# Normalized rows sent to the experts, projection by chunks and softplus by halves in the first block

## The chip, the cores and the metric

The kernel runs on one core of a Trainium2 chip. The metric is the device time of one execution in microseconds (us), the median over several. The core has five engines that run their own instruction streams in order: PE (matrix products, with weight loads shown as PEld), DVE, ACT, POOL and SP, of which SP only issues transfers here. They wait for each other on semaphores.

## The reference, cut to what matters

The input is four sequences of 1024 tokens with 512 channels. A state-space layer and a mixture of eight experts follow one another, each behind a layer norm that is modulated by per-sequence vectors, and each added back with a gate. In short:

```python
mod = silu(c) @ wmod                  # per sequence: sa, ca, ga, sb, cb, gb
h = layernorm(x) * (1 + ca) + sa
u = causal_conv(h, 4 taps) + conv_b
dt, Bm, Cm = split(u @ xproj_w.T)     # 128 + 16 + 16 columns
delta = softplus(dt @ dtproj_w.T + dtproj_b)
# 16 states per channel, step by step over the tokens
s = exp(delta * A) * s + delta * Bm * u
y = sum(s * Cm) + u * D_skip
x = x + ga * y
h = layernorm(x) * (1 + cb) + sb
logits = tanh(h @ Wg1.T) @ Wg2.T      # two of eight experts a token, softmax of the two
out = sum over both of score * (silu(h @ Wup[e].T + bup[e]) @ Wdown[e].T + bdown[e])
x = x + gb * out
```

All is 32-bit floating point.

## The kernel before, in words

**Blocks.** The tokens are cut into nine blocks (`BLOCKS`): seven of 512 tokens, then one of 384 and one of 128, the last sequence being cut 512, 384, 128. Token tiles have 128 rows; the 512 channels are four chunks (`dc`). A block goes through three parts.

*Front* (`front`): rows are loaded, normalized, turned channel-first with PE transposes, modulated (`turned`, `affine`: multiply by one column, add another) and convolved on DVE (`conv`). `u` is the convolution's output, one chunk after another. The projection `u @ xproj_w.T` (L716) gives 160 columns for each token tile; two tiles share a bank of PSUM. It is done tile by tile, each over the four chunks, and the planner's step waits for all chunks. Then `pre(dc)` makes the parts of the softplus with Abs, Exp and Identity on ACT, and one step does the four `Ln` (L838) when all four chunks are there. `post(dc)` multiplies delta by u and turns the product token-first (`duT`).

*Scan.* For each of 16 states and four chunks a unit is run: `products_b` (dB, ACT or POOL), `inputs` (PE transposes to `pb`), `decays` (Exp on ACT, L916), `recurrences` (the scan on DVE, L946), `products_c` (hc on POOL, L963), `sums` (PE, accumulated in the two banks `acc0` and `acc1`, L1002). That makes 576 units.

*Back* (`back`): the second norm on rows (`second_norm`: `xn`, token-first, and `h2T`, turned and modulated), the router on `h2T`, and positions for both choices of each token in a table of rows in DRAM, ordered by expert. `scatter(t)` turns the modulated `h2T` back to rows (L1316), copies them twice, on ACT (L1320) and on DVE (L1324), puts the score of a choice into column 512 of each copy (L1326), and writes each with an indirect transfer from POOL (L1331). Once a group's rows have landed, `tiles` loads tiles of 128 rows and the weights of their expert (1 MB each), and `expert` computes: rows turned channel-first (L1403), one copy to `xT` (helper `copy`, L347 on ACT or L349 on DVE), up product (L1416), bias, Tanh, product, down product (L1444), scaled by score and gate (L1454), stored back in place. `combine` gathers both results of each token (L1493) and adds. There are six groups of blocks (`GROUPS`), 86 tiles in all. The last block of 128 tokens goes through all eight experts densely (`dense`).

**The order.** All parts are generators. A planner written in Python (`Order`) runs them when the program is built: each `yield step(engine, cost, dependencies)` is placed where its engine is free and its inputs are there by assumed costs (`t_mm`, `t_act`, `t_dve`, `t_pool`), and due times (`DUE`, `TILES_DUE`) break ties. What it decides is the fixed order of every engine's instructions; `either` lets it choose DVE or ACT for an operation. Buffers are rings (`ring(tag, n)`): `t512B` has four row buffers, shared by `xn` and by the copies for the scatter. A cost in the planner is an assumption: it changes the order alone.

The scatter's issue as it stands:

```python
yield step(POOL, 1.2, copied, kb=256)
nc.gpsimd.tensor_copy(idx[:, k, t : t + 1], to[:, k, t : t + 1])
i = nc.gpsimd.indirect_dma_start(out=xs_d[g], out_offset=..., in_=h2[k].t, in_offset=None)
```

Of the kernel before, what the change touches and what calls it, by code (L numbers as in the profile page):

```python
# [14 lines left out]
P = 128  # L15
# [5 lines left out]
DC = D // P  # L21
# [254 lines left out]
def adaln_mamba_moe_kernel(  # L276
# [232 lines left out]
    def mod_part(s):  # L509
        if s >= 3:  # L510
# [3 lines left out]
            wm_in[s].t = o.fin  # L514
        yield step(PE, t_mm(512), banks, wm_in[s])
        pm, tag = new_bank(f"pm_{s}")
        for kc in range(DC):
            if kc:
                yield step(PE, t_mm(512))
            nc.tensor.matmul(  # L520
                pm[:B, :],
                lhsT=sc[:, kc, :],
                rhs=wm_sb[s].t[:, kc * D : (kc + 1) * D],
                start=(kc == 0),
                stop=(kc == DC - 1),
            )
# [115 lines left out]
    def front(blk):  # L642
# [61 lines left out]
        bT = Buf("bT", 2, [P, NT, NS], f"bT_{blk}")  # L704
        bT_sb[blk] = bT
        for t2 in range(0, nt, 2):
            w = min(2, nt - t2)
            yield step(PE, t_mm(XP, DC), banks, gated_in[b], *u_in)
            if t2 == 0:
                hT.done()  # L710
            px, tag = new_bank(f"pxd_{blk}_{t2}")
            for i in range(w):
                if i:
                    yield step(PE, t_mm(XP, DC))
                for kc in range(DC):
                    nc.tensor.matmul(  # L716
                        px[:, i * XP : (i + 1) * XP],
                        lhsT=u(kc)[:, (t2 + i) * P : (t2 + i + 1) * P],
                        rhs=xpg[b].t[:, kc, :],
                        start=(kc == 0),  # L720
                        stop=(kc == DC - 1),
                    )
            yield either(w * XP, 1)
            copy(xd.t[:, t2 : t2 + w, :].rearrange("p t w -> p (t w)"), px[:, : w * XP])
            yield step(DVE, 0.15)
            nc.vector.tensor_copy(
                bT.t[:, t2 : t2 + w, :], px[:, : w * XP].rearrange("p (t w) -> p t w", w=XP)[:, :, R : R + NS]
            )
            banks.give(tag, o.fin)
        if t0 + n == L:  # L730
# [19 lines left out]
        y_in = [Event() for _ in range(DC)]  # L750
        ln_in = Event()

# [25 lines left out]
        def post(dc):  # L778
            yield step(both(n), None, ln_in, y_in[dc], ring("t512A", 4))
            dd = delta[dc // 2].t[:, dc % 2, :n]  # L780
# [33 lines left out]
        for dc in range(2):  # L814
            o.spawn(pre(dc), due0 + 60.0 + 4.0 * dc, 3.0)

        yield step(PE, t_tr(nt), banks, ring("t512A", 4))
# [16 lines left out]
        for dc in range(2, DC):  # L834
            o.spawn(pre(dc), due0 + 60.0 + 4.0 * dc, 3.0)
        yield step(ACT, t_act(n, DC) + 2.6, *y_in)
        for dc in range(DC):
            nc.scalar.activation(y.t[:, dc, :n], y.t[:, dc, :n], AF.Ln, bias=1.0)  # L838
        ln_in.t = o.fin
        for h in range(2):  # L840
            yield step(POOL, 0.01, ring("duT", 3), after=[])
            duT.append(Buf("duT", 3, [P, NT, 2 * P], f"duT_{blk}_{h}"))
            for dc in range(2 * h, 2 * h + 2):
                o.spawn(post(dc), due0 + 95.0 + 4.0 * dc, 3.0)

# [310 lines left out]
    def second_norm(blk):  # L1156
        b, t0, n = BLOCKS[blk]
        nt = n // P
        x1_in = [event("x1", blk, dc) for dc in range(DC)]
        yield step(POOL, 0.01, ring("wideB", 1), ring("t512B", 4).many(nt), *x1_in)  # L1160
        h2T = wide("B", f"h2T_{blk}")
        xn = [t512("B", f"xn_b{blk}_{t}", DC) for t in range(nt)]
        yield from layernorm([[half.t[:, t, :] for half in xr[blk]] for t in range(nt)], xn, x1_in[-1], f"b{blk}", "B")
        h2_in = [Event() for _ in range(DC)]

        def turn(dc):
            yield from turned(xn, n, dc, b, 3, 4, h2T.t[:, dc, :n], f"b{blk}")
            h2_in[dc].t = o.fin

        for dc in range(DC):  # L1170
            o.spawn(turn(dc), DUE[blk + 1] + 8.0 + 2.0 * dc + LAST[blk], 2.0)
        return h2T, h2_in

    def back(blk):
# [4 lines left out]
        if b not in gbh:  # L1179
            yield from gate(b)  # L1180
        hb, h2_in = yield from second_norm(blk)
        h2T = hb.t[:, :, :n]
        rank, sv, s_all = yield from router(blk, h2T, h2_in)
        routed = Event()
# [116 lines left out]
        nc.vector.tensor_tensor(to, to, posf, ALU.add)  # L1301
        yield step(POOL, 0.55)
        idx = tl(blk, "idx", [P, 2, NT], I32, bufs=2)
        idx_sb[blk] = tl(blk, f"idx{blk}", [P, 2, NT], I32)
        nc.gpsimd.tensor_scalar(idx_sb[blk][:, :, :nt], posf, Z, None, ALU.min)
        idx_rest[blk] = tl(blk, f"idr{blk}", [P, 2, NT], I32)
        nc.gpsimd.tensor_scalar(idx_rest[blk][:, :, :nt], to, Z, None, ALU.max)
        xs_d[g] = xs_buf[g % N_XS]
        left = [nt]

        def scatter(t):
            yield step(PE, t_tr(DC), banks, ring("t512B", 4).many(2), combined[g - N_XS])
            h2 = [t512("B", f"h2_{blk}_{t}_{k}") for k in range(2)]
            ph, tag = new_bank(f"ph_{blk}_{t}")
            for dc in range(DC):
                nc.tensor.transpose(ph[:, dc * P : (dc + 1) * P], h2T[:, dc, t * P : (t + 1) * P], ident)  # L1316
            turned_in = Event()
            turned_in.t = o.fin
            yield step(ACT, t_act(512))
            nc.scalar.copy(h2[0].t[:, :D], ph)  # L1320
            copied = Event()
            copied.t = o.fin
            yield step(DVE, t_dve(512) + 0.15, after=[turned_in])
            nc.vector.tensor_copy(h2[1].t[:, :D], ph)  # L1324
            for k in range(2):
                nc.vector.tensor_copy(h2[k].t[:, D:], sv[:, k, t : t + 1])  # L1326
            banks.give(tag, o.fin)
            for k in range(2):
                yield step(POOL, 1.2, copied, kb=256)
                nc.gpsimd.tensor_copy(idx[:, k, t : t + 1], to[:, k, t : t + 1])  # L1330
                i = nc.gpsimd.indirect_dma_start(  # L1331
                    out=xs_d[g],
                    out_offset=bass.IndirectOffsetOnAxis(ap=idx[:, k, t : t + 1], axis=0),
                    in_=h2[k].t,
                    in_offset=None,
                )
                apart(f"token{g}", i)
                h2[k].done()
            left[0] -= 1
            if left[0] == 0:  # L1340
                hb.done()
                scattered[g][0] -= 1
# [52 lines left out]
    def expert(g, j, xs, w, left):  # L1395
# [6 lines left out]
        for dc in range(DC):  # L1402
            nc.tensor.transpose(px[:, dc * P : (dc + 1) * P], xs.t[:, dc * P : (dc + 1) * P], ident)  # L1403
        yield either(512, 1)
        copy(xT.t.rearrange("p c t -> p (c t)"), px)
        banks.give(tag, o.fin)
# [105 lines left out]
    def dense(blk):  # L1512
# [3 lines left out]
        for tag in ("acc0", "acc1"):  # L1516
            banks.give(tag, o.fin)
        hb, h2_in = yield from second_norm(blk)
        h2T = hb.t[:, :, :n]
# [207 lines left out]
```

## Time and profile before

| | us |
|---|---|
| median of 3 runs (lowest, highest) | 1458.58 (1455.88, 1464.79) |
| the profiled execution | 1464.0 |
| its span, from the first instruction to the last | 1462.3 |
| first scan begins | 65.0 |
| last scan ends | 1383.2 |
| busy PE / DVE / ACT / POOL | 1231.8 / 1145.7 / 1045.8 / 1045.1 |
| granted TensorE clock, mean over the span | 0.925 |

An engine's busy time is the time in which it works on at least one instruction. Lines such as `L353 ACT ACTIVATE hT<-pt_a,mod 128x128 ... x4 | 1.7, 449 | 2.2` give the line of the program, the engine, the operation, output and inputs, shape and count, then the group's busy time in us and the mean duration of one in ns, then the idle time of the engine just before and what ended it. In a timeline the first two numbers are start and duration in us; brackets hold the wait before, and what ended it. `SPq` is the transfer queue of SP.

### The profile page before, as it was taken

What the parts mean: (1) busy time and instruction counts of PE and PEld (TensorE: products, weight loads), DVE (VectorE), ACT (ScalarE), POOL (GpSimd) and SP (SyncE); (2) the same over time, 40 slices, a digit from 0 to 9 for tenths busy, and PEclk for the clock granted to TensorE, in tenths of its full rate; (3) what the DMA queues carried; (4) which work ended last, traced back from release to release, by engine and by line L of the source; (5) the groups of instructions that cost most, each with busy time, mean ns of one, the idle gap of its engine ahead of it and who ended that gap; (6) DMA issues with size and microseconds to landing.
All of it is one profiled execution on the core that took longest, in us unless ns stands there. A gap on an engine that the chain in (4) does not pass through costs nothing. (4 is left out here: it accounts for less than half of the span.)

```text
span 1462.3 us, 24472 instructions
## 1 busy us (share of the span) xinstructions
PE 1231.8 (84%) x7716; PEld 929.7 (64%) x7716; DVE 1145.7 (78%) x1861; ACT 1045.8 (72%) x2095; POOL 1045.1 (71%) x1241
## 2 busy tenths in 40 slices
PE   5588778877779989997879989998899899987886
PEld 2447565655568767775667757776677767753563
DVE  4569989898988789998896869898879888656343
ACT  2779898689778676899686766896789868444320
POOL 1468987798788567897796657787788878656222
PEclk8799988889899999999798999999999999996798
DMA  4357663847599999653788976777999978966997
GB/s 176 112 158 158 120 170 83 210 109 205 124 271 281 284 266 253 216 144 97 200 280 279 289 219 209 248 248 199 290 281 286 282 196 318 339 182 158 343 311 206
DMA packets 141935, 321.65 MB, mean 220 GB/s; under 512 B 14899, under 2 KB 43475, under 8 KB 128998
## 3 DMA queue, kind: packets, MB, share of 16 engines
q1 hardware_dynamic: 111344, 254.35, 57.0%
q0 software_dynamic: 13888, 32.58, 10.4%
q10 hardware_dynamic: 16566, 33.08, 8.9%
q8 instruction: 63, 1.03, 0.3%
q14 instruction: 74, 0.61, 0.1%
HBM read 245.95 MB, written 82.40 MB: 225 GB/s over the span
## 5 line engine op out<-in xcount | busy, mean ns | idle before, releaser
L963 POOL TENSOR_TENSOR hc<-h,cq 128x512 f32<-128x512 f32 (+2 forms) x576 | 685.1, 1259 | 184.0 <-PE acc L1002 57.1
L888 ACT ACTIVATE dB<-duT,bT 128x256 f32<-128x256 f32 x820 | 368.1, 499 | 85.3 <-PE pb L931 79.9
L931 PE MATMUL pb<-ident,dB 128*128 128x128 f32 x2048 | 348.1, 293 | 82.5 <-DVE h L946 66.9
L916 ACT ACTIVATE h<-delta,a_neg 128x512 f32<-128x512 f32 (+2 forms) x576 | 369.7, 666 | 61.1 <-POOL state L971 30.7
L1002 PE MATMUL acc<-ident,hc 128*128 128x128 f32 x2048 | 340.4, 291 | 69.0 <-POOL hc L963 67.0
L946 DVE TENSOR_TENSOR_SCAN h<-h,state,pb 128x512 f32<-128x512 f32 (+2 forms) x320 | 330.4, 1054 | 50.3 <-PE pb L931 24.9
L931 PEld LDWEIGHTS pb<-ident,dB 128*128 128x128 f32 x2048 | 252.5, 150 | 171.1 <-DVE h L946 86.2
L1002 PEld LDWEIGHTS acc<-ident,hc 128*128 128x128 f32 x2048 | 251.2, 148 | 153.9 <-POOL hc L963 110.0
L946 DVE TENSOR_TENSOR_SCAN h<-h,pb 128x512 f32<-128x512 f32 x256 | 303.5, 1208 | 51.7 <-PE pb L931 32.3
L1444 PE MATMUL po<-w,hid 128*128 128x512 f32 x344 | 182.7, 621 | 9.9 <-DVE hid L1436 9.8
L1416 PE MATMUL pe<-xT,w 128*128 128x128 f32 x1376 | 183.9, 278 | 3.4 <-ACT xT L347 3.4
L1416 PEld LDWEIGHTS pe<-xT,w 128*128 128x128 f32 x1376 | 170.2, 193 | 25.8 <-issue 13.3
L895 POOL TENSOR_TENSOR dB<-duT,bT 128x512 f32<-128x512 f32 (+1 forms) x108 | 109.4, 1044 | 30.5 <-PE pb L931 24.6
L1493 POOL DMA_INDIRECT xc<-xs,idx x56 | 90.3, 1613 | 44.9 <-DMA xc<-xs,idx 18.3
L1454 DVE SCALAR_TENSOR_TENSOR xs<-po,xs,gbh 128x512 f32<-128x512 f32 x86 | 63.8, 742 | 42.9 <-PE po L1444 42.6
L1331 POOL DMA_INDIRECT xs<-h,idx x62 | 63.5, 1024 | 35.1 <-POOL idx L1330 12.3
L1434 ACT ACTIVATE th<-pe 128x256 f32<-128x256 f32 x86 | 32.5, 378 | 66.1 <-DVE pe L1427 65.6
L1444 PEld LDWEIGHTS po<-w,hid 128*128 128x128 f32 x344 | 55.4, 198 | 26.1 <-issue 16.6
L347 ACT COPY xT<-px 128x512 f32<-128x512 f32 x81 | 46.7, 578 | 31.8 <-PE px L1403 31.6
L971 POOL COPY state<-h 128x2 f32<-128x2 f32 x160 | 56.0, 350 | 0.0
L1403 PE MATMUL px<-ident,xs 128*128 128x128 f32 x344 | 54.4, 283 | 1.2 <-DVE delta L774 1.2
L1427 DVE TENSOR_TENSOR pe<-pe,w 128x256 f32<-128x256 f32 x86 | 36.1, 420 | 22.9 <-PE pe L1416 19.3
(200 smaller groups left out, 1523.2 us busy)
## 6 DMA issues: line engine op xcount, KB each, us to landing
w<-w_all SPq DMA_DIRECT2D x86, 1025.0 KB, 9.4
cq<-scr SPq DMA_DIRECT2D x224, 256.0 KB, 4.8
xs<-xs SPq DMA_DIRECT2D x86, 256.5 KB, 5.3
xs<-xs SPq DMA_DIRECT2D x86, 256.0 KB, 8.3
xs<-xc ACTq DMA_DIRECT2D x16, 1026.0 KB, 9.9
we<-w_all SPq DMA_DIRECT2D x8, 1025.0 KB, 14.5
xf<-in_x SPq DMA_DIRECT2D x32, 256.0 KB, 5.6
xr<-in_x SPq DMA_DIRECT2D x14, 512.0 KB, 10.7
```

What stands on the lines that cost most here:

```text
L888: nc.scalar.activation(dB[u // 2].t[:, t, :], duT_sb[blk][half].t[:, t, :], AF.Identity, scale=bT_sb[blk].t[:, t, n : n + 1],)
L895: engine().tensor_tensor(dB[u // 2].t[:, t0:t1, :], duT_sb[blk][half].t[:, t0:t1, :], bT_sb[blk].t[:, t0:t1, n].unsqueeze(2).to_broadcast( ...
L916: nc.scalar.activation(hs[u // 2].t[:, i, :ln], delta_sb[blk][half].t[:, i, :ln], AF.Exp, scale=a_neg[:, dc, n : n + 1])
L931: nc.tensor.transpose(pbs[u][:, t * P : (t + 1) * P], dB[u // 2].t[:, t, i * P : (i + 1) * P], ident)
L946: nc.vector.tensor_tensor_scan(h, h, pbs.pop(u)[:, :ln], 0.0 if t0 == 0 else state[:, n, dc : dc + 1], ALU.mult, ALU.add,)
L963: nc.gpsimd.tensor_tensor(hcs[u].t[:, :ln], hs[u // 2].t[:, i, :ln], cq[u // 2].t[:, :ln], ALU.mult)
L1002: nc.tensor.matmul(acc[blk, dc][:, t * P : (t + 1) * P], lhsT=src.t[:, t * P : (t + 1) * P], rhs=ident, is_transpose=True, start=False, st ...
L1331: i = nc.gpsimd.indirect_dma_start(out=xs_d[g], out_offset=bass.IndirectOffsetOnAxis(ap=idx[:, k, t : t + 1], axis=0), in_=h2[k].t, in_off ...
L1416: nc.tensor.matmul(pu[:, hc * P : (hc + 1) * P], lhsT=up[:, kc, hc * P : (hc + 1) * P], rhs=xT.t[:, kc, :], start=(kc == 0), stop=(kc == D ...
L1444: nc.tensor.matmul(po, lhsT=hid.t[:, hc * P : (hc + 1) * P], rhs=w.t[:, W_DN + hc * D : W_DN + (hc + 1) * D], start=(hc == 0), stop=(hc == ...
L1454: nc.vector.scalar_tensor_tensor(xs.t[:, :D], po, xs.t[:, D:], gbh[b].t, ALU.mult, ALU.mult)
L1493: nc.gpsimd.indirect_dma_start(out=a, out_offset=None, in_=xs_d[g], in_offset=bass.IndirectOffsetOnAxis(ap=idx_sb[blk][:, choice, t : t + ...
```

## The change

Three things are changed.

1. In the first block the projection loops over channel chunks outside and token tiles inside: each chunk is used as soon as its convolution is done. It accumulates in the two banks `acc0` and `acc1`, which the scans do not use yet. Also, the planner's cost of the first modulation product (`s == 0`) is doubled.
2. In the first block `Ln` is done for two halves of the channels, each with its own event, and the `post` of a half is started behind it. In all blocks the `Ln` of several chunks is one instruction: 1024 columns in the first block, 2048 in the others (fewer in short blocks).
3. The rows that are scattered are the normalized rows `xn` themselves. The turn back, both copies and the small index casts go. POOL writes the score of a choice into column 512 of `xn` and issues the transfer, for choice 0 and then for choice 1 from the same buffer. The index table is cast once a block. In `expert` the modulation is applied when the turned tile is copied to `xT`: four `affine` operations of 128 columns in place of one copy of 512. `xn` is held until it is scattered, `h2T` only until the router is done.

The diff, cut to its core:

```diff
@@ mod_part
-        yield step(PE, t_mm(512), banks, wm_in[s])
+        slow = 2 if s == 0 else 1
+        yield step(PE, t_mm(512, slow), banks, wm_in[s])
...
@@ front
+        pxs = []
+        if blk == 0:
+            for t2 in range(0, nt, 2):
+                pxs.append(psum.tile([P, 512], F32, tag=f"acc{t2 // 2}", name=f"pxd_{blk}_{t2}"))
+            for kc in range(DC):
+                yield step(PE, t_mm(XP, nt), gated_in[b], u_in[kc])
+                for t in range(nt):
+                    nc.tensor.matmul(
+                        pxs[t // 2][:, t % 2 * XP : (t % 2 + 1) * XP],
+                        lhsT=u(kc)[:, t * P : (t + 1) * P],
+                        rhs=xpg[b].t[:, kc, :],
+                        start=(kc == 0 and t % 2 == 0),
+                        stop=(kc == DC - 1 and t % 2 == 1),
+                    )
...
+        LN = 2 if blk == 0 else 1
+        ln_in = [Event() for _ in range(LN)]
+
+        def logs(k):
+            c0, c1 = k * DC // LN, (k + 1) * DC // LN
+            yield step(ACT, t_act(n * (c1 - c0)) + 2.6, *y_in[c0:c1])
+            nc.scalar.activation(y.t[:, c0:c1, :n], y.t[:, c0:c1, :n], AF.Ln, bias=1.0)
+            ln_in[k].t = o.fin
+
+        def posts(h):
+            yield step(POOL, 0.01, ring("duT", 3), after=[])
+            duT.append(Buf("duT", 3, [P, NT, 2 * P], f"duT_{blk}_{h}"))
+            for dc in range(2 * h, 2 * h + 2):
+                o.spawn(post(dc), due0 + 95.0 + 4.0 * dc, 3.0)
...
+        if LN == 2:
+            o.spawn(logs(0), due0 + 64.0, 3.0)
+            yield from posts(0)
...
-        yield step(ACT, t_act(n, DC) + 2.6, *y_in)
-        for dc in range(DC):
-            nc.scalar.activation(y.t[:, dc, :n], y.t[:, dc, :n], AF.Ln, bias=1.0)
-        ln_in.t = o.fin
...
+        yield from logs(LN - 1)
+        for h in range(LN - 1, 2):
+            yield from posts(h)
@@ second_norm
-        xn = [t512("B", f"xn_b{blk}_{t}", DC) for t in range(nt)]
+        xn = [t512("B", f"xn_b{blk}_{t}", DC + (blk + 1 < NBLK)) for t in range(nt)]
@@ back
-        yield step(POOL, 0.55)
+        yield step(POOL, 0.8)
...
+        nc.gpsimd.tensor_copy(idx[:, :, :nt], to)
...
         def scatter(t):
-            yield step(PE, t_tr(DC), banks, ring("t512B", 4).many(2), combined[g - N_XS])
-            h2 = [t512("B", f"h2_{blk}_{t}_{k}") for k in range(2)]
...
-                nc.tensor.transpose(ph[:, dc * P : (dc + 1) * P], h2T[:, dc, t * P : (t + 1) * P], ident)
...
-            nc.scalar.copy(h2[0].t[:, :D], ph)
...
-            nc.vector.tensor_copy(h2[1].t[:, :D], ph)
             for k in range(2):
-                nc.vector.tensor_copy(h2[k].t[:, D:], sv[:, k, t : t + 1])
...
-                yield step(POOL, 1.2, copied, kb=256)
-                nc.gpsimd.tensor_copy(idx[:, k, t : t + 1], to[:, k, t : t + 1])
+                yield step(POOL, 1.3, combined[g - N_XS], kb=256)
+                nc.gpsimd.tensor_copy(xn[t].t[:, D:], sv[:, k, t : t + 1])
                 i = nc.gpsimd.indirect_dma_start(
...
-                    in_=h2[k].t,
+                    in_=xn[t].t,
...
@@ expert
-        yield either(512, 1)
-        copy(xT.t.rearrange("p c t -> p (c t)"), px)
+        yield either(P, DC)
+        for dc in range(DC):
+            affine(xT.t[:, dc, :], px[:, dc * P : (dc + 1) * P], mcol(4, dc, b), mcol(3, dc, b))
```

More of the change, by code (lines that the diff above doesn't have):

```diff
@@ L518, in mod_part @@
             if kc:
-                yield step(PE, t_mm(512))
+                yield step(PE, t_mm(512, slow))
             nc.tensor.matmul(
@@ L705, in front @@
         bT_sb[blk] = bT
+        pxs = []
[12 more added lines that the diff above has]
+                    )
+            hT.done()
+            pxs_in = Event()
+            pxs_in.t = o.fin
         for t2 in range(0, nt, 2):
             w = min(2, nt - t2)
[L708 to L712, printed above, removed]
+            if blk:
+                yield step(PE, t_mm(XP, DC), banks, gated_in[b], *u_in)
+                if t2 == 0:
+                    hT.done()
+                px, tag = new_bank(f"pxd_{blk}_{t2}")
+            else:
+                px = pxs[t2 // 2]
+            for i in range(w if blk else 0):
                 if i:
@@ L722, in front @@
                     )
-            yield either(w * XP, 1)
+            if blk:
+                yield either(w * XP, 1)
+            else:
+                yield either(w * XP, 1, after=[pxs_in])
             copy(xd.t[:, t2 : t2 + w, :].rearrange("p t w -> p (t w)"), px[:, : w * XP])
@@ L728, in front @@
             )
-            banks.give(tag, o.fin)
+            if blk:
+                banks.give(tag, o.fin)
         if t0 + n == L:
@@ L750, in front @@
         y_in = [Event() for _ in range(DC)]
-        ln_in = Event()
+        LN = 2 if blk == 0 else 1
[10 more added lines that the diff above has]
+                o.spawn(post(dc), due0 + 95.0 + 4.0 * dc, 3.0)
         def pre(dc):
@@ L778, in post @@
         def post(dc):
-            yield step(both(n), None, ln_in, y_in[dc], ring("t512A", 4))
+            yield step(both(n), None, ln_in[dc * LN // DC], y_in[dc], ring("t512A", 4))
             dd = delta[dc // 2].t[:, dc % 2, :n]
@@ L835, in front @@
             o.spawn(pre(dc), due0 + 60.0 + 4.0 * dc, 3.0)
-        yield step(ACT, t_act(n, DC) + 2.6, *y_in)
-        for dc in range(DC):
-            nc.scalar.activation(y.t[:, dc, :n], y.t[:, dc, :n], AF.Ln, bias=1.0)
-        ln_in.t = o.fin
[L840 to L844, printed above, removed]
+        yield from logs(LN - 1)
+        for h in range(LN - 1, 2):
+            yield from posts(h)
     UNITS = []
@@ L1171, in second_norm @@
             o.spawn(turn(dc), DUE[blk + 1] + 8.0 + 2.0 * dc + LAST[blk], 2.0)
-        return h2T, h2_in
+        return h2T, h2_in, xn
     def back(blk):
@@ L1180, in back @@
             yield from gate(b)
-        hb, h2_in = yield from second_norm(blk)
-        h2T = hb.t[:, :, :n]
-        rank, sv, s_all = yield from router(blk, h2T, h2_in)
+        hb, h2_in, xn = yield from second_norm(blk)
+        rank, sv, s_all = yield from router(blk, hb.t[:, :, :n], h2_in)
+        hb.done()
         routed = Event()
@@ L1311, in scatter @@
         def scatter(t):
-            yield step(PE, t_tr(DC), banks, ring("t512B", 4).many(2), combined[g - N_XS])
-            h2 = [t512("B", f"h2_{blk}_{t}_{k}") for k in range(2)]
[L1314 to L1324, printed above, removed]
-            for k in range(2):
-                nc.vector.tensor_copy(h2[k].t[:, D:], sv[:, k, t : t + 1])
-            banks.give(tag, o.fin)
-            for k in range(2):
-                yield step(POOL, 1.2, copied, kb=256)
-                nc.gpsimd.tensor_copy(idx[:, k, t : t + 1], to[:, k, t : t + 1])
+            for k in range(2):
+                yield step(POOL, 1.3, combined[g - N_XS], kb=256)
+                nc.gpsimd.tensor_copy(xn[t].t[:, D:], sv[:, k, t : t + 1])
                 i = nc.gpsimd.indirect_dma_start(
@@ L1337, in scatter @@
                 apart(f"token{g}", i)
-                h2[k].done()
+            xn[t].done()
             left[0] -= 1
             if left[0] == 0:
-                hb.done()
                 scattered[g][0] -= 1
@@ L1517, in dense @@
             banks.give(tag, o.fin)
-        hb, h2_in = yield from second_norm(blk)
+        hb, h2_in, _ = yield from second_norm(blk)
         h2T = hb.t[:, :, :n]
```

## The prediction

> **What bounds the kernel now.** I read the page first, then busy time by stretches, then groups by form, then the timeline of the start and of the end.
>
> ```profile
> span 1462.3 us, 24472 instructions
> PE 1231.8 (84%) x7716; PEld 929.7 (64%) x7716; DVE 1145.7 (78%) x1861; ACT 1045.8 (72%) x2095; POOL 1045.1 (71%) x1241
> ```
>
> Four engines lie between 71% and 84%: no single one bounds the whole. The stretches below run from the first scan of a half block to that of the next (columns: span, then busy time of PE, PEld, DVE, ACT, POOL, clock, DMA).
>
> ```profile
> 193.00:270.00 77.00, 59.15 (x352) 44.04 (x352) 70.52 (x124) 64.19 (x125) 60.52 (x69) 0.88 0.49 118
> ...
> 574.00:641.00 67.00, 62.95 (x446) 51.56 (x445) 62.10 (x73) 57.99 (x112) 56.99 (x49) 1.00 0.74 221
> 641.00:722.00 81.00, 65.71 (x385) 47.22 (x383) 71.22 (x133) 65.72 (x131) 63.99 (x84) 0.87 0.49 125
> ...
> 908.00:975.00 67.00, 64.37 (x456) 52.35 (x455) 61.30 (x71) 59.66 (x117) 52.71 (x44) 1.00 0.77 240
> ...
> 1069.00:1137.00 68.00, 63.05 (x446) 52.74 (x445) 60.11 (x72) 61.06 (x127) 61.19 (x63) 0.95 0.91 278
> ```
>
> Two kinds are seen. Where a block's second half (norm, router, scatter) runs and almost no expert tile does (193 to 270, 332 to 411, 641 to 722), DVE is fullest, 70.5 of 77. Where expert tiles run, PE is, 63 to 64 of 67, and ACT stands at 58 to 61. From 65 to 1383 us scans follow one another with four pauses over 10 us (20 the longest), so what the start saves and what each stretch saves adds up.
>
> **The change, part by part.** The sum is made against the profiled execution, 1464.0 us (span 1462.3 and 1.7 around it). The median of the runs shown is 1458.6, that is 5.4 lower; I forecast the difference and take it from the median.
>
> *The start.* The timeline:
>
> ```profile
> 34.54 6.20 PE L716 MATMUL pxd<-xpg,u 128*128 128x160 f32 x26 [0.55 <-DVE u L684]
> ...
> 40.77 0.42 ACT L347 COPY xd<-pxd 128x320 f32<-128x320 f32 x1 [2.74 <-PE pxd L716]
> ...
> 50.93 1.28 ACT L838 ACT_TABLE_LOAD   x1
> 52.23 2.19 ACT L838 ACTIVATE y<-y 128x512 f32<-128x512 f32 x4
> ...
> 62.91 1.28 ACT L916 ACT_TABLE_LOAD   x1
> ...
> 64.96 1.22 DVE L946 TENSOR_TENSOR_SCAN h<-h,pb 128x512 f32<-128x512 f32 x1 [5.00 <-ACT h L916]
> ```
>
> (a) Six of 32 projection instructions run before the last conv chunk is there (34.5); 26 stand behind it, 6.2/26 = 0.238 us each. By chunks they start at the first chunk (29.8), and 32 x 0.238 = 7.6 ends at 37.4 instead of 40.7: -3.3. Bounds -1 (first pairs took 0.9, so PE may run slower here) to -4.3 (only the last chunk's eight left after 34.5). (b) The doubled planning cost of the first modulation product takes no device time, but orders: now the fourth row tile's statistics stand on DVE behind a copy that waits for PE until 14.89, though the third ended at 13.1. The norm can come 1.7 sooner, but convolution also needs the gate (23.9). I take -1.0, bounds 0 to -1.7. (c) Softplus by halves: the first log can run after the third chunk's Exp and Identity, at 50.3, and its half ends at 50.3 + 1.28 + 1.05 = 52.6. Then one post per engine (1.27 + 1.5), the turn (0.9), its copy (0.6): duT at about 57 where the second copy now ends at 61. ACT has two more table loads before the first decay: 50.3 + 1.28 + 1.05 + 1.28 + 1.2 + 1.28 + 1.05 = 57.4, two duT copies 1.0, load and Exp 2.0, one dB 0.8: scan at 61.2 instead of 64.96. Of these 3.7 about 1.2 comes back, because the second half's copies fall into the first scans (ACT 56.0 of 65 there). -2.5, bounds +2.6 (both loads paid, the half ordered too late to gain) to -4. Start: **-6.8**, bounds +1.6 to -10.
>
> For (c) a rule speaks against it. The Trainium skill (ScalarE: Activation LUTs, What ACT_TABLE_LOAD costs) puts a switch of sets at 2.66 us, a drain being added to the load. Here the load at 50.93 begins 0.02 us after Identity ends and the log follows it at 52.23, so the trace shows 1.28 and no drain. By the rule two more switches would cost 5.3, (c) would come to about zero, and the sum would be 2.8 less of a gain.
>
> *Scatter.* Per token tile four transposes, two copies of 512 and small ones go:
>
> ```profile
> L347 ACT COPY xT<-px 128x512 f32<-128x512 f32 x81 | 46.7, 578 | 31.8 <-PE px L1403 31.6
> ...
> L1316 PE MATMUL ph<-ident,h2T 128*128 128x128 f32 x124 | 24.7, 337 | 6.7 <-DVE xr L1199 3.3 <-DVE pick L1290 1.0 <-DVE xs L1454 0.8
> ...
> L1324 DVE COPY h<-ph 128x512 f32<-128x512 f32 x31 | 21.2, 684 | 14.6 <-ACT h L1320 8.1 <-DMA xs<-h,idx 5.8
> ...
> L1320 ACT COPY h<-ph 128x512 f32<-128x512 f32 x31 | 18.0, 580 | 16.2 <-PE ph L1316 15.2 <-DMA xs<-h,idx 0.8
> ...
> L353 ACT ACTIVATE hT<-pt_a,mod 128x128 f32<-128x128 f32 x4 | 1.7, 449 | 2.2 <-PE pt_a L610 2.2
> ```
>
> DVE loses 0.61 + 2 x 0.06 = 0.73 a tile start to start, PE 24.7/31 = 0.8, ACT 0.48. In the three stretches that DVE bounds, 12 tiles: 12 x 0.73 = -8.8; several of these scatters fall into the next stretch, so **-7** (0 to -11, the latter with idle time before the copies). Nineteen tiles lie where experts run: 19 x 0.8 = 15 us less on PE, of which I count half, because a turn's four run in 0.44 when nothing stops them: **-8** (0 to -15).
>
> *The wait added.* Both choices now leave from one buffer, so POOL's score copy for choice 1 waits until the scatter of choice 0 has read it. That DMA lands 3.2 to 13.0 us after issue, median 6.4; the plan spaces the two steps 7.0 apart. Queued behind it on POOL stand hc products, then acc sums and the h ring. Two in five land later than that, by 2.2 on average: 31 x 0.4 x 2.2 = 27 of POOL waiting. Of the 35 that POOL idles before L1331, the 12 behind the cast stay and some 18 behind DVE and ACT go, and what remains is partly POOL's slack. The score copies replace 62 casts of 0.23 one for one. **+3**, bounds -5 to +16.
>
> *The tile.* One copy becomes four affine operations of 128 columns. Nearest row: 449 ns, and 0.345 start to start where two stand in a row; 4 x 0.345 - 0.47 = 0.91 more, x86 = 78 on ACT (the planner may move some to DVE, at 0.4 each by the 128-wide row there). Against it 9 from scatter copies and 2 from logs merged four into one: net 67. Cover: ACT's idle time in expert stretches, 230 + 615 us of them, 630 busy. The plan books 1.19 for what should take 1.4 to 1.5. No stretch now runs ACT above 0.90; were that the ceiling, stretches with 5 to 7 tiles (574, 908, 1069, and slightly 411) would grow by 2.5 + 4.4 + 7 + 1 = 15. I take half, since the plan can hand dB to POOL: **+8**, bounds 0 to +67.
>
> *The end.* The last group's rows:
>
> ```profile
> 1342.05 1.00 POOL L1331 DMA_INDIRECT xs<-h,idx  x1 [0.28 <-POOL idx L1330]
> ...
> 1349.29 0.32 SPq L1376 DMA_DIRECT2D xs<-xs  x1
> ...
> 1402.46 4.53 SPq L1538 DMA_DIRECT2D we<-w_all  x3
> ...
> 1416.72 1.49 PE L1546 MATMUL pue<-h2T,we 128*128 128x128 f32 x11 [1.99 <-DMA we<-w_all]
> ```
>
> Six scatters run from 1320 to 1342, paced by transposes, copies and buffers; SP's tile loads wait for the last to land. Straight from the normalized rows they fit into 1319 to 1330 (1.3 each, a pause for the shared buffer), so ten tiles start up to 12 us sooner. The dense block's weights at 1402 follow; but its h2T is there only at 1405, so at most 1416.7 - 1407 = 9.7 is won. **-7**, bounds 0 to -9.7.
>
> Sum: -6.8 - 7 - 8 + 3 + 8 - 7 = **-17.8**: 1446.2 for the profiled execution, 1440.8 against the median.
>
> **The rivals.** *A, all covered:* ACT's 67 us fit into its idle time, start and end give their best: -10 - 11 - 15 - 9.7 = -46, 1413. For: of ACT's idle time 80 us is waiting for PE before dB. Against: in-order queues rarely hide everything.
>
> *B, PE was not the bound:* The expert stretches give nothing for 15 us of PE, and ACT takes its ceiling: -6.8 - 7 + 0 + 3 + 15 - 7 = -2.8, 1455.8. For: weight loads in 574 to 641 are busy 51.6 of 67 only. Against: PE itself shows 62.95 of 67. The Trainium skill (Trainium Kernel Development and Optimization, Performance Expectations) says that matmul busy time misleads and that LDWEIGHTS busy time is to be read; by it this case would be the likeliest.
>
> *C, slower:* ACT becomes the bound. In-order, the four operations of a tile stand before decays and dB, which scans wait for already (39.1 us behind L916, the most after PE's 57.2). Without ACT's term the gains are 25.8; the 67 cancel them from 39% uncovered on and pass 1% slower from 60%. At 70%: +47 - 26 = +21, 1480. For: ACT at 61 of 68 with seven tiles, which bring 6.4 more. Against: the stretches with the back parts have ACT at 66 to 71 of 94 to 103.
>
> *D, it doesn't do what it says:* the planner puts the first logs behind all exponentials, and the shared buffer keeps scatters as slow; then (c) and the end give nothing: -8, 1450. Within B's range.
>
> **How the numbers follow.** Forecast 0.45, its own range 1427 to 1451; A 0.12; B and D 0.21; C 0.22. One per cent, 1444.0 and 1473.2, is about what a measurement tells from no change. Faster: 0.34 of the forecast, A, 0.02 of B and D: 0.48. Same: 0.11 + 0.19 = 0.30. Slower: C, 0.22. The range 1415 to 1480 leaves out half of A and about half of C.
>
> **What would show it.** First scan near 58 instead of 65, two more table loads; no ph group; xT affine near 0.35 to 0.45 each, mostly ACT; stretch 1069 no longer than 72; the last group's six scatters within 14 us. ACT over 0.92 in stretches that have grown, with PE waiting for xT, would show C; POOL idle over 20 us before score copies would show the scatter term wrong.

## The result, and the profile after

The changed kernel takes 1454.33 us (1446.27 to 1462.23, 20 runs) where the kernel before takes 1462.99 beside it: a ratio of 0.9943, 95% interval 0.9924 to 0.9962. It is faster by 8.3 us; the forecast was 17.8. Its profiled execution took 1449.1 us. The page's first lines:

```profile
span 1447.4 us, 24237 instructions
...
PE 1218.5 (84%) x7592; PEld 920.1 (64%) x7592; DVE 1145.1 (79%) x1801; ACT 1089.1 (75%) x2264; POOL 1048.7 (72%) x1248
```

The work moved as the diff says: 124 PE transposes and 60 DVE instructions fewer, 43 us more of ACT. ACT alone is clearly fuller, 75% for 72%; PE stays the fullest, at 84%. In parts of the span (us; the last stage runs from block 8's first scan to the end):

| | first scan | blocks 0 to 7 | block 8 and the tail |
|---|---|---|---|
| before | 65.0 | 1210.2 | 187.1 |
| after | 62.3 | 1206.8 | 178.3 |
| forecast of the difference | -6.8 | -4 | -7 |
| measured, one profile each | -2.7 | -3.4 | -8.8 |

Single profiled executions lie up to some 6 us off their kernel's median (before's 1464.0 is on the high side, after's 1449.1 on the low). The three differences add up to -14.9 where the kernels differ by 8.3, so the middle column can't be read to better than that. The last column repeats: the last stage takes 180.0 to 181.2 in three more profiles of the changed kernel, and 185.7 to 191.5 in five profiles with the order of the kernel before. The first column repeats in part: in those three profiles the first scan begins at 62.6 to 64.6, so against 65.0 the start gains between 0.4 and 2.7.

The stretches by half blocks of the changed kernel (columns: span, then busy time of PE, PEld, DVE, ACT, POOL, clock, DMA), which answer to 193, 574, 641, 805, 908 and 1069 of before:

```profile
188.30:265.90 77.60, 60.93 (x332) 43.21 (x330) 69.23 (x115) 62.17 (x122) 61.36 (x73) 0.79 0.56 126
569.70:636.40 66.70, 63.17 (x456) 52.27 (x455) 61.49 (x75) 59.88 (x120) 56.46 (x48) 1.00 0.75 224
636.40:716.70 80.30, 63.85 (x370) 46.02 (x368) 70.62 (x127) 64.33 (x132) 64.52 (x87) 0.83 0.50 133
804.20:900.00 95.80, 82.75 (x496) 60.92 (x495) 80.82 (x138) 70.26 (x146) 67.12 (x78) 0.89 0.72 221
900.00:968.40 68.40, 65.93 (x477) 54.71 (x476) 62.81 (x77) 62.57 (x125) 58.79 (x50) 1.00 0.73 228
1057.70:1131.60 73.90, 63.92 (x458) 51.90 (x457) 68.95 (x78) 64.32 (x138) 62.38 (x65) 1.00 0.90 254
```

Of the stretches with a back part, where the removed transposes and copies had been, two hardly changed: 77.6 for 77.0 and 80.3 for 81.0. The one from 804 to 900 is 6.7 shorter, but it also issues 105 matmuls fewer, of which the removed transposes are 16: expert tiles have moved out of it. A pair of neighbours shows where such tiles went, first before, then after:

```profile
332.00:411.70 79.70, 57.84 (x352) 42.48 (x352) 69.68 (x132) 63.88 (x125) 61.65 (x85) 0.89 0.69 169
411.70:479.10 67.40, 61.68 (x448) 52.71 (x447) 58.48 (x70) 56.93 (x108) 60.42 (x68) 0.97 0.92 282
```

```profile
325.90:401.40 75.50, 59.73 (x318) 41.11 (x317) 68.83 (x122) 58.91 (x119) 60.54 (x85) 0.79 0.70 171
401.40:476.60 75.20, 71.67 (x511) 60.49 (x510) 62.39 (x76) 66.57 (x136) 59.59 (x64) 0.98 0.97 305
```

The first of the two, with the back part, is 4.2 shorter with 34 matmuls fewer; the one behind it is 7.8 longer with 63 more. Between 193 and 1138 of the kernel before, its six stretches with a back part take 531.3 us together and 511.6 in the changed kernel, with 265 matmuls fewer; the six behind them take 414.1 and 431.7, with 174 more. Three more profiles of each order show the same: 507 to 509 against 531 to 541, and 433 to 435 against 413 to 417. The stretch at 1057, forecast at no more than 72, has 73.9. ACT is fullest at 62.57 of 68.40, 0.915.

### The profile page after: what moved, and what is told of

Read it like the earlier page. It is cut to its first block, busy times and chain, and to the rows that moved or that the text cites. A ratio compares the mean times of both kernels' runs of the same rounds, so it can differ in the third digit from the quotient of the medians.

```text
span 1447.4 us, 24237 instructions
## 1 busy us (share of the span) xinstructions
PE 1218.5 (84%) x7592; PEld 920.1 (64%) x7592; DVE 1145.1 (79%) x1801; ACT 1089.1 (75%) x2264; POOL 1048.7 (72%) x1248
## 5 line engine op out<-in xcount | busy, mean ns | idle before, releaser
L1038 PEld LDWEIGHTS acc<-ident,hc 128*128 128x128 f32 x2048 | 254.1, 149 | 157.7 <-POOL hc L999 122.5
L1438 PE MATMUL pe<-xT,w 128*128 128x128 f32 x1376 | 189.9, 284 | 3.1 <-ACT xT L353 1.9
L1438 PEld LDWEIGHTS pe<-xT,w 128*128 128x128 f32 x1376 | 177.2, 199 | 19.2 <-issue 10.1
L1466 PE MATMUL po<-w,hid 128*128 128x512 f32 x344 | 179.6, 611 | 7.4 <-DVE hid L1458 7.0
L931 POOL TENSOR_TENSOR dB<-duT,bT 128x512 f32<-128x512 f32 (+1 forms) x113 | 113.7, 1042 | 35.6 <-PE pb L967 27.0
L353 ACT ACTIVATE xT<-px,mod 128x128 f32<-128x128 f32 x312 | 116.5, 457 | 29.3 <-PE px L1424 28.7
L1353 POOL DMA_INDIRECT xs<-xn_b,idx x62 | 62.7, 1011 | 18.0 <-POOL xn_b L1352 13.9
L1007 POOL COPY state<-h 128x2 f32<-128x2 f32 x160 | 63.3, 396 | 0.0
L1449 DVE TENSOR_TENSOR pe<-pe,w 128x256 f32<-128x256 f32 x86 | 36.0, 418 | 22.0 <-PE pe L1438 19.9
```

Source lines behind the costliest of these rows:

```text
L353: nc.scalar.activation(dst, src, AF.Identity, bias=bias, scale=scale)
L931: engine().tensor_tensor(dB[u // 2].t[:, t0:t1, :], duT_sb[blk][half].t[:, t0:t1, :], bT_sb[blk].t[:, t0:t1, n].unsqueeze(2).to_broadcast( ...
L1038: nc.tensor.matmul(acc[blk, dc][:, t * P : (t + 1) * P], lhsT=src.t[:, t * P : (t + 1) * P], rhs=ident, is_transpose=True, start=False, st ...
L1438: nc.tensor.matmul(pu[:, hc * P : (hc + 1) * P], lhsT=up[:, kc, hc * P : (hc + 1) * P], rhs=xT.t[:, kc, :], start=(kc == 0), stop=(kc == D ...
L1466: nc.tensor.matmul(po, lhsT=hid.t[:, hc * P : (hc + 1) * P], rhs=w.t[:, W_DN + hc * D : W_DN + (hc + 1) * D], start=(hc == 0), stop=(hc == ...
```

## The experiments

Each run has a ratio to the kernel before, timed in the same set on the same chip. Two of the five sets ran where every kernel, the one before included, took some 20 us longer (before: 1478.8 and 1477.3, against 1458.3, 1459.3 and 1455.2), so times are compared only within a set, and ratios across them.

**The changed kernel again, three times**, as the measure for its variants.

> The changed kernel itself, beside its variants on one chip, so that each is read against it. Both theories expect about what was measured: 6 to 11 us below the kernel before, first scan at 62 us in the trace.

> The changed kernel again, since the last chip was slower for all (the kernel before took 1479 us there): does its gain of 0.5% hold beside other variants? Theory 1: 6 to 11 us below the kernel before on any chip. Rival (the gain is of the same size as what any reordering does, and depends on the granted clock): within 4 us.

> The changed kernel on the same chip as the rows' part alone. Theory 1 (the gain is the program's): 6 to 11 us below the kernel before, whether that takes 1460 or 1478 us here. Rival (on a chip with a lower granted clock the gain is smaller): within 4 us, if the kernel before takes over 1475 us here.

Ratios 0.9949 (0.9919 to 0.9979), 0.9932 (0.9905 to 0.9958) and 0.9940 (0.9914 to 0.9967). The gain stands.

**The start: the doubled cost taken out.** The first scan came 4 us later than the forecast of 58. The timeline of the changed kernel shows where:

```profile
6.42 7.75 PE L521 MATMUL pm<-wm,sc 128*4 128x512 f32 x12 [6.42 <-DMA wm<-in_wmod]
...
17.89 0.09 PEld L521 LDWEIGHTS pm<-wm,sc 128*4 128x4 f32 x2 [4.64 <-DMA wm<-in_wmod]
17.89 1.60 PE L521 MATMUL pm<-wm,sc 128*4 128x512 f32 x2 [3.71 <-ACT xf L353]
19.42 0.58 PE L536 MATMUL pmt<-ident,mrow 4*128 4x4 f32 x4
...
20.05 0.17 DVE L543 COPY mod<-pmt 128x16 f32<-128x16 f32 x1 [5.82 <-PE pmt L536]
...
33.77 7.01 PE L715 MATMUL pxd<-xpg,u 128*128 128x160 f32 x32 [5.74 <-DVE u L685]
...
40.27 0.97 ACT L347 COPY xd<-pxd 128x320 f32<-128x320 f32 x2 [9.14 <-PE pxd L715]
...
50.23 1.28 ACT L783 ACT_TABLE_LOAD   x1
...
52.60 1.28 ACT L809 ACT_TABLE_LOAD   x1
...
55.17 1.28 ACT L783 ACT_TABLE_LOAD   x1
```

In the kernel before, the four little transposes of the first modulation vector (`pmt`) stood on PE from 14.44 on:

```profile
14.44 0.41 PE L535 MATMUL pmt<-ident,mrow 4*128 4x4 f32 x4
```

Now they come at 19.42, behind a matmul of the third product, whose weights land only at 17.9: its weight load (PEld, 17.89) waits 4.64 us for that transfer. All of the first block follows.

```diff
-        slow = 2 if s == 0 else 1
+        slow = 1
```

> The changed kernel with the planned cost of the first modulation product not doubled (slow = 1); every engine's order is that of the changed kernel but for some 15 instructions at the start. Theory 1 (the shortfall of the forecast sits in the start): the doubled cost put the third product's first matmul, whose weights land at 17.9 us, ahead of the first product's turn on PE; without it modulation is back at the times of the kernel before (14.9, 19.9, 22.8 us), the first scan begins at 57 to 58 us instead of 62.3, and the time falls by 4 to 5 us against the changed kernel, since nothing behind it changes. Rival (the start's gain is taken back by the first scans or later, and the shortfall lies in ACT's extra work): the first scan comes earlier, but the time stays within 2 us of the changed kernel.

By the traces the order changes at the start alone: the four transposes stand ahead of the third product's first matmul again, and one `hT` operation goes from ACT to DVE. Its timeline:

```profile
13.84 0.40 PE L536 MATMUL pmt<-ident,mrow 4*128 4x4 f32 x4
...
14.28 0.17 DVE L543 COPY mod<-pmt 128x16 f32<-128x16 f32 x1 [1.11 <-PE pmt L536]
...
17.61 1.88 PE L521 MATMUL pm<-wm,sc 128*4 128x512 f32 x4 [1.55 <-DMA wm<-in_wmod]
...
29.75 7.17 PE L715 MATMUL pxd<-xpg,u 128*128 128x160 f32 x32 [5.09 <-DVE u L685]
...
36.41 0.97 ACT L347 COPY xd<-pxd 128x320 f32<-128x320 f32 x2 [8.83 <-PE pxd L715]
```

The vector is ready at 14.28 and not 20.05, projection begins 4.0 sooner, and the first scan at 58.4. Ratio 0.9931 (0.9904 to 0.9958): a median of 1446.0 against 1450.2 of the changed kernel in the same set. The scan's 6 us are shown (58.4 for 64.5 in that set); the time's 4 are likely only, since the intervals overlap.

**The same with the true landing time.** The planner takes the third product's weights to be there at 14; here it is told 18, and the doubled cost stays.

```diff
-        wm_in[s].t = 6.0 + 4.0 * s
+        wm_in[s].t = (6.0, 10.0, 18.0)[s]
```

> The changed kernel with the planner told that the third product's weights are there at 18 us instead of 14; orders differ from the changed kernel's in some ten instructions at the start. Theory 1 (the doubled cost did harm only because this landing was assumed too early): the first product's turn stands before the third product on PE, first scan at 57 to 59 us, 12 to 15 us below the kernel before, that is 4 to 6 below the changed one. Rival: no more than 2 us below the changed kernel.

The three vectors stand at 14.54, 19.37 and 24.51 (after: 20.05, 24.73 and 27.48), and the first scan begins at 59.1. So for the scan it was the false landing time, which only the doubled cost brought to bear. The time did not follow as expected: the ratio is 0.9950 (0.9929 to 0.9972), in a set where before takes 1477, 7 us below it and not 12 to 15, and no better than the changed kernel's ratios in other sets. The changed kernel itself does not stand beside it; what the earlier scan is worth in time rests on the plain cost alone.

**Does a late start carry to the end?** Before's order, with 52 small ACT copies put ahead of the work.

```diff
+    for _ in range(52):
+        nc.scalar.copy(a_exp, ones[:, : DC * NS])
```

> The kernel before with all orders kept and some 50 small copies on ACT ahead of its first use in the modulation, which hold the start back. Theory 1 (time at the start goes through to the end): first scan 4 to 8 us later, the time longer by as much, to within 2 us. Rival (what the start gains or loses is made up behind it, by transfers, by the clock or by the slack of the engines): the time longer by less than half of the delay of the first scan.

First scan at 77.4, 12.4 later than in the first profile; ratio 1.0071 (1.0038 to 1.0104), +10.4 us. With the order kept, most of a start's delay is in the time.

**The first block's parts alone**, twice: chunks and halves with the plain cost, rows as before.

> The parts in the first block alone (projection by chunks, softplus by halves, logs merged), with the planned cost of the first modulation product not doubled; rows go to the experts as before. Theory 1 (what the first scan wins goes through to the end): first scan at 58 to 59 us, time 5 to 7 us below the kernel before. Rival (it is taken back in the blocks behind): first scan as early, time within 3 us of the kernel before.

> The first block's parts alone once more, without the doubled cost, on another chip. Theory 1 (the start goes through, as a late start went through by 10 of 12 us): first scan at 58.4, 5 to 7 us below the kernel before. Rival (the order of everything behind the start is another one, 854 of 2247 lines of PE's order differ, and it loses as much): within 3 us of it.

First scan at 58.4 and 58.6, and yet no gain: 1.0010 (0.9988 to 1.0031) and 1.0019 (0.9994 to 1.0044), both in the slower sets. The planner re-planned all that follows: 854 of 2247 lines of PE's order differ from before's. The 6.6 us of the start were given back behind it; where, the runs don't show.

**The rows alone**, three times: before's first block with the third part of the change.

> The third part of the change alone (normalized rows scattered, modulated in the tile); the first block is as before. Theory 1 (the start of the changed kernel gave next to nothing because of the doubled cost, and all of its gain is from this part): 5 to 9 us below the kernel before. Rival (the first block's part carries the gain, the rows pay for themselves at most): within 3 us of the kernel before.

> The third part alone once more, on another chip. Theory 1 (the rows' part carries the changed kernel's gain, and the slower chip hid it): 5 to 9 us below the kernel before. Rival (alone it is worth nothing, because the order that the planner finds for it loses in the expert stretches what the back parts and the end win): within 3 us of it.

> The third part alone on the same chip as the changed kernel. Theory 1 (alone it is worth nothing; the order that goes with the changed first block is a better one): within 3 us of the kernel before, on any chip. Rival (the chip decided): 5 to 9 us below the kernel before, if that takes under 1465 us here.

1.0003 (0.9979 to 1.0027) and 0.9999 (0.9971 to 1.0028) in the slower sets, 0.9971 (0.9941 to 1.0000) in a faster one: 0 to -4 us, where the terms of the prediction for this part come to -11. In the faster set the changed kernel stood beside it and was 2.3 us lower by the medians. The last group's six scatters leave within 12 to 14 us here too, but the last stage takes 189.5 and 190.2 in the slower sets (191.5 in the kernel before there) and 180.9 in the faster one.

**The four affine operations.** First one copy in their place, with all orders kept:

```diff
-        for dc in range(DC):
-            affine(xT.t[:, dc, :], px[:, dc * P : (dc + 1) * P], mcol(4, dc, b), mcol(3, dc, b))
+        copy(xT.t.rearrange("p c t -> p (c t)"), px)
```

> The changed kernel with every engine's order kept, but the four affine operations of an expert tile replaced by the one copy of before: the modulation of the expert rows is left out, and about 78 us of ACT's work with it. Theory 1 (the added work on ACT is mostly hidden, 8 of 67 us come through): 5 to 12 us below the changed kernel. Rival (ACT's work is what ate the gain): 20 us or more below it.

then each of them twice:

```diff
-        for dc in range(DC):
+        for dc in range(2 * DC):
+            dc = dc % DC
```

> The changed kernel with every engine's order kept, but each affine operation of an expert tile done twice: eight of 128 columns instead of four, 86 x 1.38 = 119 us more on ACT and DVE. Theory 1 (about 12% of such work comes through): 10 to 30 us above the changed kernel. Rival (ACT is the bound in the expert stretches): 60 us or more above it.

The groups of the tile, in the changed kernel, with one copy and with eight operations:

```profile
L353 ACT ACTIVATE xT<-px,mod 128x128 f32<-128x128 f32 x312 | 116.5, 457 | 29.3 <-PE px L1424 28.7
...
L355 DVE TENSOR_SCALAR xT<-px,mod 128x128 f32<-128x128 f32 x32 | 10.8, 404 | 0.0
```

```profile
L347 ACT COPY xT<-px 128x512 f32<-128x512 f32 x78 | 45.0, 578 | 35.9 <-PE px L1424 35.5
```

```profile
L353 ACT ACTIVATE xT<-px,mod 128x128 f32<-128x128 f32 x624 | 226.1, 480 | 22.3 <-PE px L1424 22.1
```

One copy saves 71.5 of ACT's busy time and gives 0.9925 (0.9897 to 0.9954), a median 4.0 lower than the changed kernel's. Doubling adds 109.6 on ACT, some 119 with DVE's share, and gives 1.0269 (1.0221 to 1.0317), 45 us more. The first 72 cost about 4, with intervals that overlap, and the next 110 cost 45. That fits a change that used up nearly all of ACT's cover and went hardly beyond it; but the eight stand in an order planned for four, so a part of the 45 may be a tile's longer chain and not ACT's fullness.

**The transposes and the copies, each doubled in the kernel before**, its orders kept:

```diff
-            for dc in range(DC):
+            for dc in list(range(DC)) * 2:
```

> The kernel before with all orders kept and the four transposes ahead of each scatter done twice: 124 more, 25 us of PE's busy time, 14 us at their pace of 0.11. It prices what the change takes from PE. Theory 1 (PE bounds most stretches; about half comes through, as in the forecast): 6 to 14 us above the kernel before. Rival (PE is not the bound): within 4 us of it.

```diff
             nc.scalar.copy(h2[0].t[:, :D], ph)
+            nc.scalar.copy(h2[0].t[:, :D], ph)
...
             nc.vector.tensor_copy(h2[1].t[:, :D], ph)
+            nc.vector.tensor_copy(h2[1].t[:, :D], ph)
```

> The kernel before with all orders kept and the two copies of 512 columns ahead of each scatter done twice: 31 x 0.61 = 19 us more on DVE and 31 x 0.48 = 15 us more on ACT. It prices what the change takes from DVE and ACT there. Theory 1 (DVE bounds the stretches with a back part): 7 to 14 us above the kernel before. Rival (these copies lie under other waits): within 4 us of it.

124 more transposes (L1316's busy time 40.8 for 24.7): 1.0043 (1.0017 to 1.0069), +6.3 us. PE time in the scatter does count, at about 0.4 of itself, near the half that the prediction took. The copies: 1.0301 (1.0260 to 1.0342), +43.9 us for some 34 us of work, counted from start to start. In the timeline of that kernel a tile's steps stand in series over four engines:

```profile
254.15 0.58 ACT L1321 COPY h<-ph 128x512 f32<-128x512 f32 x1
...
254.77 0.69 DVE L1325 COPY h<-ph 128x512 f32<-128x512 f32 x1 [1.94 <-ACT h L1321]
255.50 0.69 DVE L1326 COPY h<-ph 128x512 f32<-128x512 f32 x1
...
257.19 1.27 POOL L1333 DMA_INDIRECT xs<-h,idx  x1 [2.60 <-DVE h L1328]
```

DVE idles 1.94 us for ACT's second copy, then POOL 2.60 for DVE's. Work put into an order that wasn't planned for it costs more than its length; from that it doesn't follow that taking the same copies out and planning anew gains as much, and the rows alone show that it doesn't.

**The end: the last rows held back.** The last scatter of the last group waits until the 11th unit of the last half has been scanned, about as late as before's last scatter.

```diff
+                late = [event("h", N_U - PER // 2 + 10)] if g == NG - 1 and t == nt - 1 and k == 1 else []
-                yield step(POOL, 1.3, combined[g - N_XS], kb=256)
+                yield step(POOL, 1.3, combined[g - N_XS], *late, kb=256)
```

> The changed kernel, with the last scatter of the last group held back in the plan until the eleventh unit of the last half block has been scanned, that is about 40 us before the scans end, as in the kernel before (41 us there, 64 us in the changed kernel). Theory 1 (the end is gated by the landing of the last group's rows): tile loads of the last group and the first product of the dense block come 8 to 14 us later, time 5 to 10 us above the changed kernel. Rival (the end is set by the last scans, or by weight loads): time within 3 us of it.

> The changed kernel with the last scatter of the last group held back once more, on another chip, where the changed kernel should stand 8 us below the kernel before. Theory 1 (the end is gated by the landing of those rows): 5 to 10 us above the changed kernel, so 3 us below to 2 us above the kernel before. Rival: as the changed kernel, 6 to 10 us below.

The end in the changed kernel, and then with the row held back:

```profile
1320.91 0.98 POOL L1353 DMA_INDIRECT xs<-xn_b,idx  x1 [0.28 <-POOL xn_b L1352]
...
1328.52 0.32 SPq L1397 DMA_DIRECT2D xs<-xs  x1
...
1399.72 4.93 SPq L1560 DMA_DIRECT2D we<-w_all  x5
...
1406.29 1.94 PE L1568 MATMUL pue<-h2T,we 128*128 128x128 f32 x15 [0.29 <-DMA we<-w_all]
```

```profile
1351.77 1.05 POOL L1354 DMA_INDIRECT xs<-xn_b,idx  x1 [0.28 <-DVE h L982]
...
1359.00 0.32 SPq L1398 DMA_DIRECT2D xs<-xs  x1
...
1424.35 1.84 PE L1569 MATMUL pue<-h2T,we 128*128 128x128 f32 x15
```

The group's first tile load comes 7.6 and 7.2 us after the last row's issue, and the dense block's first product comes later with it. The last stage takes 190.0 and 189.1, as in the kernel before. The ratios are 1.0023 (0.9997 to 1.0050) and 0.9994 (0.9976 to 1.0013), both in the slower sets, where the changed kernel was not run. The fair comparison is with the true-landing kernel in the second set, whose rows are not held back: its last stage takes 181.9, and it is 6.6 us faster. Its first scan too is 4.5 sooner; if that passes on as in the late start (10.4 of 12.4), it is worth up to 3.8 of the 6.6, so the end by itself is worth 3 to 7, an estimate.

**The kernel before, profiled again** in a slower set.

> The kernel before once more, for a second profile of it: its first profile was of an execution some 5 us above the median. Both theories expect no difference in time; in the trace the first scan at 65 us, and blocks 0 to 7 some 5 us shorter than the 1210 us of the first profile.

```profile
span 1479.9 us, 24472 instructions
...
PE 1248.6 (84%) x7716; PEld 942.5 (64%) x7716; DVE 1145.0 (77%) x1861; ACT 1047.3 (71%) x2095; POOL 1047.3 (71%) x1241
```

Ratio 0.9995 (0.9974 to 1.0017). Against its first profile the span is 17.6 longer and PE's busy time 16.8, at a clock of 0.911 for 0.925; DVE, ACT and POOL are as busy as before to 2.2 us. The clock is not what tells the sets apart, though: over all runs of the kernel before it is 0.919 in the slower sets and 0.922 to 0.924 in the others, and at 0.921 single runs took 1459.4 in one of the faster and 1479.0 in one of the slower.

## Why the prediction was right in direction and wrong in size

The direction was right; the gain was 8.3 us where 17.8 were forecast. By the prediction's own limit of one per cent that is no change that a measurement tells apart, which had a chance of 0.30, and not a faster kernel, which had 0.48. The ratio put on its median gives 1450.3, just within the 1427 to 1451 of its main case; that is no support for the sum, since two of its terms failed. By its steps:

- **Start (a), projection by chunks: right.** Forecast to end at 37.4; without the doubled cost it begins at 29.75 and lasts 7.17, to 36.9.
- **Start (b), the doubled planning cost: this step failed.** It was put at -1.0, bounds 0 to -1.7, "takes no device time, but orders". It does order, and the fourth tile's statistics come 1.6 sooner (13.34 for 14.98), as it said. But the prediction followed only DVE's statistics and did not look at what PE would put ahead of the vector's transposes. That was a product whose weights land at 17.9. Undone, the first scan moves to 58.4, from 62.3 in the first profile and 64.5 in the same set, so (b) is +4 to +6 on the scan. In time it is some 4 in the one set that compares them, with intervals that overlap.
- **Start (c), softplus by halves: right.** From the first `dt` product to the first scan it is 22.6 us before and 19.9 after: -2.7 for -2.5.

```profile
42.36 3.70 PE L759 MATMUL pd<-dt,dt_w 128*128 128x512 f32 x8 [0.24 <-ACT dt L347]
```

```profile
42.40 1.12 PE L798 MATMUL pd<-dt,dt_w 128*128 128x512 f32 x2 [0.68 <-ACT dt L347]
...
62.27 1.22 DVE L982 TENSOR_TENSOR_SCAN h<-h,pb 128x512 f32<-128x512 f32 x1 [0.96 <-ACT h L952]
```

  The table loads are the 1.28 that the prediction counted, each followed at once by its function. The Trainium skill (ScalarE: Activation LUTs, What ACT_TABLE_LOAD costs) would have 2.66 for each switch, a drain included; the trace shows no drain.
- **Scatter, -7 and -8: this term failed too, and by more.** The rows alone, with the added wait, the tile's operations and the end, give 0 to -4 for a forecast of -11. With the tile at about 4 and the end between -1.5 (by the last stage of the rows alone in the slower sets) and -9 (by that of the changed kernel), the transposes, the copies and the wait come to between -6.5 and +5, an estimate, where the sum had -15 and +3. The prediction took each stretch as it stood and counted what leaves it. The planner did not leave it so: the stretches with a back part got 19.7 us shorter and those behind them 17.6 longer. Of the 265 matmuls fewer in the former, 88 are the transposes; the 177 others, at 67.4/448 = 0.15 us each, would take 27 us by an estimate, so moved tiles are enough to explain the shortening. The doubled transposes show that PE time in the scatter does cost with the order kept, and the doubled copies that the chain does; why their removal brought so little stays open.

  One thing that goes with the removal is seen, though not isolated: a lower clock of PE. Over all runs it is 0.913 to 0.916 for the changed kernel and 0.922 to 0.924 for the kernel before in the same three sets; with the transposes doubled it is 0.927, but with the copies doubled, where PE has no work less, 0.904. The stretch in the kernel before that answers to 804 to 900 above:

```profile
805.20:907.70 102.50, 92.66 (x601) 70.29 (x600) 84.65 (x158) 71.15 (x139) 69.99 (x80) 0.97 0.78 235
```

  It had 0.97, and 0.94 to 1.00 in the six other profiles with before's rows; with the rows sent directly it is 0.86 to 0.91 in all 13. In other stretches the two kinds overlap, and in 722 to 805, with 61 matmuls more, the clock even rose, 0.90 to 0.96. The product of the scores with the experts' bias rows (`pc`), the same instruction in both, first before, then after:

```profile
L1193 PE MATMUL pc<-bdg,sT 8*128 8x512 f32 x62 | 40.1, 729 | 2.0 <-DVE h L1326 1.9
```

```profile
L1229 PE MATMUL pc<-bdg,sT 8*128 8x512 f32 x62 | 48.6, 872 | 2.2 <-DVE xs L1476 0.7 <-DVE u L685 0.7 <-DVE xr L1235 0.7
```

  It takes 813 to 915 ns in the 13 profiles, and 699 to 782 in six of the seven; in the seventh, with the copies doubled, 885. The shortest and the longest are the same before and after, 587 and 1217 ns; it is the mean that moves. That group alone takes back 8.5 of the 24.7 us that the transposes left, and PE's busy time fell by 13.3 only.
- **The wait added, +3: right in place, smaller in size.** POOL's score copies wait 9 times for the scatter from the shared buffer, 9.5 us in all, where 27 were expected; the transfers land in 2.9 to 11.0 us, median 8.2.
- **The tile, +8: about half, if the 4 holds.** The work is what was forecast (457 and 404 ns an operation), its price about 4, with intervals that overlap.
- **The end, -7: right in place, in size within 3 to 7.** The six scatters go from 1308 to 1321 and not from 1320 to 1342, and the last stage is 6 to 9 us shorter than the 187.1 of before. The dense block's first product comes at 1406.3 for 1416.7; of these 10.4, 6.2 are the earlier start of the whole stage (1269.0 for 1275.2).

Of the rivals, *C* fell: the kernel is not slower, and ACT reaches 0.915 only. *A* fell: neither start nor scatter nor tile gave its best. *B* is borne out by half: transposes taken out gave next to nothing, as it says, though added ones cost 6.3 us; but ACT's price is near 4 and not its 15. *D* meets the time, 1450, by luck: the logs do run by halves, and the six scatters do come within 14 us. Adding up the parts fails too: the two halves of the change alone gave nothing to -4 and nothing, and together 8. In one slower set they stood side by side: the rows 0.9999, the first block 1.0019, and the whole, with the true landing time, 0.9950. The planner's order is common to all, and why the whole keeps more than its parts stays open.

## What to carry to other kernels

A number that only a planner reads is an edit like any other: ask which instruction it lets in ahead of the one that the chain waits for, on every in-order engine, and what that instruction itself waits for. Taking work out and planning anew is not the mirror of adding it with the order kept, so test a removal by a removal. And work removed from PE is priced by what its stretch and the one behind it get shorter together, since a planner may move other work from one to the other, and what stays may run slower.

## What the runs showed of the hardware

- With the scatter's transposes gone the granted clock over all runs was 0.913 to 0.916 for 0.922 to 0.924, in the stretch at 805, which also lost tiles, 0.89 for 0.97, and the same 62 matmuls took 872 ns each for 729. With 124 transposes more it was 0.927. The Trainium skill (TensorE: Matmul & The Clock Gate, Part 1) says that the throttled state is the default and that activity releases it; these figures agree in direction. One stretch does not: from 192 to 270 the doubled transposes had 13 matmuls more and a clock of 0.78 for 0.87.
- The same program takes 20 us longer in some sets than in others. In one pair of profiles PE's busy time alone grew with the span (+16.8 of +17.6), but at the same clock of 0.921 runs took 1459.4 and 1479.0; the reason stays open.
- A switch between the tables of Exp and Ln on ACT took 1.28 us, and the next function began within 0.02 us: loads at 50.23, 52.60 and 55.17.
- An affine operation of 128 columns from PSUM took ACT 457 ns, and a copy of 512 columns 578: four in place of one cost 71.5 us of busy time over 78 tiles.
- Work added on ACT in a kept order was not priced evenly: 72 us cost about 4, within noise, the next 110 cost 45.
